# Layer norms transposed by VectorE, transfers and GpSimd in place of TensorE, in a two-layer cross-attention kernel

## The chip, the cores and the metric

One core of a Trainium2 chip runs the whole kernel. Its engines are named as in the profile: PE (TensorE, matrix products; PEld is its weight load), DVE (VectorE), ACT (ScalarE), POOL (GpSimd) and SP, whose queue issues nearly all transfers here. The metric is the device time of one execution in microseconds.

## The reference

Two transformer layers over x of 4 batches, 512 tokens and 320 features, with a context of 1601 tokens and 192 features per batch, all in 32-bit floats. Each layer does, for every batch:

```python
h1 = _ln(x, n1_g, n1_b)
x = _attn(h1, h1, q1, k1, v1, o1_w, o1_b, heads) + x
h2 = _ln(x, n2_g, n2_b)
x = _attn(h2, context, q2, k2, v2, o2_w, o2_b, heads) + x
h3 = _ln(x, n3_g, n3_b)
proj = h3 @ ff_w1 + ff_b1
a, g = jnp.split(proj, 2, axis=-1)
ff = a * jax.nn.gelu(g, approximate=False) @ ff_w2 + ff_b2
return ff + x
```

`_ln` subtracts the mean over the 320 features, divides by the standard deviation, and applies a gain and a bias per feature. `_attn` has 20 heads of 16 features: queries, keys and values are products, the scores are softmaxed over the keys, and the heads' outputs go through one more product. The feed-forward part has 2 x 1280 columns in its first product and 1280 rows in its second.

## The kernel before, in words

The work is cut into units in one fixed list: per layer, 20 self-attention units (4 batches by 5 groups of 4 heads), 20 cross-attention units, and 4 feed-forward units, one a batch. An attention unit goes through its keys in chunks of 128, 4 chunks in self and 13 in cross. For each chunk PE forms the scores of four heads (tile `st`, line 1185), ACT raises them to exponentials (`pr`, line 1195), and PE multiplies them with the values (`av`, line 1211); ACT copies the result out and POOL adds it up in `o` (line 1231). Each unit needs the largest score of every query beforehand: PE forms the scores a second time in another layout (`sps`, lines 959 and 986) and DVE takes their maxima (`pm` or `nmax`, lines 974 and 996). These products for the next units are woven into the score products of the present one, or are given out as extra rounds.

Everything else a unit needs (norms, projections of queries, keys and values, output products) stands in chains, queues of small steps with a cost and a due time counted in rounds. A round is half a chunk in attention. After each chunk `steps` takes the most urgent heads of the chains, as far as a credit allows. Steps marked `LIGHT` are limited to one or two at a time. The order of instructions on each engine is so written out when the program is built; on the chip every engine goes through its own list in order. Transfers of queries, keys and other things are queued and issued by `carry`, a few each round.

A layer norm is one run of the chain `norm`, 24 of them (2 layers, 3 places, 4 batches). DVE forms mean and variance of four tiles of 128 tokens (line 533), an inverse root is found by Newton steps on POOL (lines 503 to 513), DVE normalises each tile into `hn` (line 550), and then `turn` has PE transpose `hn` against an identity, three pieces of features by four tiles, 12 transposes a norm, into a PSUM bank `hps` (line 564). ACT reads each bank, applies gain and bias and writes `hT`, the normalised input with features on partitions (line 573). POOL adds the next product's bias to x (line 579). `hT` has two buffers; a buffer may be overwritten when the norm two before has been read by all its products (`may_overwrite`). For feed-forward norms the last 64 features are normalised twice, so that they lie on both halves of the partitions.

`hT` is the moving operand of the projections (lines 791, 832) and of the first feed-forward product (line 1314, and line 1328 for the last 64 features), and the stationary one for self-attention's values (line 920). The product that ends an attention (`ops`, line 1114) takes the heads' outputs `aT` by tiles of tokens.

The first cross unit of a layer is called early: its projections are put into the chains `AHEAD` = 8 units ahead, and its maxima are given out as extra rounds while self units still run (`giver`). In the last unit before the feed-forward part the next unit has no maxima, so ACT's exponentials set its pace.

Of the kernel before, what the change touches and what calls it, by code (L numbers as in the profile page):

```python
# [20 lines left out]
FF = 4 * D  # L21
# [13 lines left out]
DK = [(0, 0, 112), (1, 112, 112), (2, 224, 96)]  # L35
CK = [(0, 0, 96), (1, 96, 96)]
# [11 lines left out]
AHEAD = 8  # L48
# [5 lines left out]
REST = D - 2 * P  # L54
NAMES = (
# [18 lines left out]
def kernel(ctx: ExitStack, tc: tile.TileContext, x, context, ws, out):  # L74
# [83 lines left out]

    def take_weights():
        room["w1r"] = shared.tile([P, FF], F32, tag="rests", name="w1r")  # L160
        room["w2"] = shared.tile([P, NHC, D], F32, tag="second", name="w2")
# [19 lines left out]
    wqk = wpool.tile([P, 3, G, 2, GD], F32, name="wqk")  # L181
    wq1, wk1 = (wqk[:, :, :, i, :] for i in range(2))
# [22 lines left out]
    def load_rows(t, w, chunks):  # L205
        return [lambda k=k, at=at, n=n: dma(out=t[:n, k, :], in_=w[at : at + n, :]) for k, at, n in chunks]

    def load_columns(t, v, chunks):
        with nc.allow_non_contiguous_dma(reason="a vector's elements go to partitions"):
            for k, at, n in chunks:  # L210
                dma(out=t[:n, k : k + 1], in_=v[at : at + n].rearrange("(p o) -> p o", o=1))
# [10 lines left out]
    def load_norm(l, i):  # L222
        for t, v in ((lng[i], ws[l][f"n{i + 1}_g"]), (lnb[i], ws[l][f"n{i + 1}_b"])):
            load_columns(t, v, FK if i == 2 else DK)
# [4 lines left out]
    def load_self(l):  # L229
        return [lambda: load_norm(l, 0)] + [  # L230
            f for t, n in ((wq1, "q1"), (wk1, "k1"), (wv1, "v1")) for f in load_rows(t, ws[l][n], DK)
# [10 lines left out]
    def load_cross(l):  # L242
        def rows(t, w):
# [7 lines left out]
            + load_rows(wq2, ws[l]["q2"], DK)  # L251
# [4 lines left out]
    def load_ff(l):  # L256
# [5 lines left out]
        def last_rows(half):  # L262
            dma(
                out=room["w1r"][half * REST : (half + 1) * REST, :],
                in_=ws[l]["ff_w1"][2 * P :, half * FF : (half + 1) * FF],
# [4 lines left out]
            [small]  # L270
            + [lambda half=half: last_rows(half) for half in range(2)]
            + [lambda c=c: dma(out=room["w2"][:, c], in_=second[:, c]) for c in range(NHC)]
# [3 lines left out]
    def load_first(l):  # L276
# [3 lines left out]
            lambda k=k, at=at, c=c: dma(out=w1[:, k, c : c + n], in_=ws[l]["ff_w1"][at : at + P, c : c + n])  # L280
            for k, at, _ in FK
            for c in range(0, 2 * FF, n)
# [89 lines left out]
    chains = {n: deque() for n in ("divide", "project", "norm", "context", "early", "proj", "values")}  # L372
    clock = {"round": 0, "credit": 0.0, "lights": 0, "tiles": None}
# [141 lines left out]
    hn_used = []  # L515


    readers = []
# [5 lines left out]
    def add_norm(l, b, i, put, done, due):  # L524
# [20 lines left out]
        def normalise(t):  # L545
            if t == 0:
                s["hn"] = one.tile([P, NQ, D + REST], F32, tag="hn", name="hn")

            for to, at, n in ((0, 0, D), (D, D - REST, REST))[: 1 + i // 2]:
                nc.vector.tensor_scalar(  # L550
                    s["hn"][:, t, to : to + n], xb[:, t, at : at + n],
                    s["mv"][:, t, 0:1], s["rstd"][:, t : t + 1], ALU.subtract, ALU.mult,
                )
            busy("dve", 0.4 * (1 + i // 2))
            s["round"] = clock["round"]

        def turn(k, at, n):
            if k == 0:
                s["hT"] = two.tile([P, 3, N], F32, tag="hT", name="hT")
                readers.append(done)  # L560
            ps = bank("hps")
            n += REST if n == REST else 0
            for t in range(NQ):
                nc.tensor.transpose(ps[:n, t * P : (t + 1) * P], s["hn"][:, t, at : at + n], ident)  # L564
            written(0.5, ps)
            busy("act", 0.7, ps)
            if start["on"] and k == 1:
                nc.vector.tensor_scalar(
                    s["hT"][:n, k, :], ps[:n, :],
                    lng[i][:n, k : k + 1], lnb[i][:n, k : k + 1], ALU.mult, ALU.add,  # L570
                )
            else:
                nc.scalar.activation(
                    s["hT"][:n, k, :], ps[:n, :], AF.Identity,
                    bias=lnb[i][:n, k : k + 1], scale=lng[i][:n, k : k + 1],
                )
            for t in ((0,), (1,), (2, 3))[k]:

                nc.gpsimd.tensor_tensor(xb[:, t, :], xb[:, t, :], brow[(3 * l + i) % 2], ALU.add)
# [1016 lines left out]
```

## Time and profile before

| | us |
|---|---|
| runs, median of 3 | 3007.71 (3005.52 to 3010.42) |
| the profiled execution | 3006.85 |
| its span, first to last instruction | 3005.1 |
| PE busy | 2902.2 (97%) |
| DVE busy | 2115.8 (70%) |
| ACT busy | 1921.5 (64%) |
| POOL busy | 1158.6 (39%) |

The six stages, read from the times at which the groups of instructions change: self-attention of layer 0 up to 375 us, cross-attention up to 1236, feed-forward up to 1545; the same for layer 1 up to 1870, 2720 and 3005. In a row of a group of instructions, the line and engine come first, then what is written and read, the shapes and the count; after the bar the busy time and the mean duration of one, and after the next bar the idle time of the engine just before, with what ended it. In a row of the timeline the first number is the start and the second the time from the first start to the last end of a run of like instructions.

### The profile page before, as it was taken

The numbers are of one execution on the slowest core, as the hardware profiler recorded it, in microseconds if no ns is written. First come the engines' busy times: TensorE is split into PE (matmuls) and PEld (weight loads), VectorE is DVE, ScalarE is ACT, GpSimd is POOL, SyncE is SP. The second block draws the span as 40 slices with busy tenths as digits, with TensorE's granted clock in tenths as the row PEclk, the third lists the DMA queues.
The fourth block names the chain that finished last, engine by engine and source line by source line (L and its number), as shares of the span: only waits on it lengthen the run. The fifth ranks groups of instructions, "written<-read, shape, count | busy, mean of one in ns | idle before, by whom it ended". The sixth has DMA issues, their size and how long they took to land.

```text
span 3005.1 us, 84209 instructions
## 1 busy us (share of the span) xinstructions
PE 2902.2 (97%) x35210; PEld 1529.1 (51%) x35210; DVE 2115.8 (70%) x4061; ACT 1921.5 (64%) x3780; POOL 1158.6 (39%) x1257
## 2 busy tenths in 40 slices
PE   8999999999999999999999999999999999999999
PEld 4455554555554555455554555545545545544555
DVE  6877888888888888322257778888888888873221
ACT  3766677877877878511147666788778778784110
POOL 3444344454544444201124443444454444442000
PEclk9999999999999999999999999999999999999999
DMA  4454233132132121300123332221221121213000
GB/s 111 100 129 99 67 79 83 45 90 56 37 93 59 38 57 27 94 6 0 33 52 74 96 97 65 70 55 42 53 60 40 49 61 43 55 22 89 10 11 14
DMA packets 165548, 177.13 MB, mean 59 GB/s; under 512 B 72484, under 2 KB 116272, under 8 KB 165168
## 3 DMA queue, kind: packets, MB, share of 16 engines
q1 hardware_dynamic: 164376, 170.56, 22.5%
q8 instruction: 277, 4.54, 0.6%
q10 hardware_dynamic: 760, 1.18, 0.2%
q14 instruction: 103, 0.84, 0.1%
q0 software_dynamic: 32, 0.00, 0.0%
HBM read 55.76 MB, written 29.36 MB: 28 GB/s over the span
## 4 chain that ended last, share of the span: by engine, by line
PE 58%; DVE 8%; POOL 1%; issue 1%; ACT 0%; DMA 0%; SPq 0%; ACTq 0%; POOLq 0%; DVEq 0%
PE av L1211 14%; PE st L1185 10%; PE fps L1314 9%; PE yps L1371 6%; DVE pm L974 5%; PE sps L959 4%; PE vps L920 3%; PE fps L1328 2%; PE ops L1114 2%; PE kps L856 2%; PE qkps L791 2%; DVE nmax L974 2%; PE qps L832 1%; PE sps L986 1%; PE hps L564 1%
## 5 line engine op out<-in xcount | busy, mean ns | idle before, releaser
L1195 ACT ACTIVATE pr<-st 128x512 f32<-128x512 f32 (+1 forms) x2720 | 1404.8, 605 | 400.7 <-PE st L1185 359.4
L974 DVE TENSOR_REDUCE pm<-sps 128x1 f32<-128x512 f32 x1920 | 1186.9, 681 | 158.1 <-PE sps L959 150.1
L1231 POOL TENSOR_TENSOR o<-o,vo 128x512 f32<-128x512 f32 x576 | 740.3, 1285 | 1185.2 <-ACT vo L1230 1157.1
L959 PE MATMUL sps<-kT,q 32*128 32x512 f32 x4800 | 874.5, 429 | 15.2 <-DMA q<-low 5.6
L1211 PE MATMUL av<-pr,vals 128*32 128x512 f32 (+1 forms) x5440 | 738.2, 607 | 64.1 <-DVE pm L974 11.9
L1185 PE MATMUL st<-q,kT 32*128 32x512 f32 (+1 forms) x5120 | 783.7, 421 | 2.4 <-DVE pm L974 1.6
L1185 PEld LDWEIGHTS st<-q,kT 32*128 32x128 f32 (+1 forms) x5120 | 417.8, 180 | 273.1 <-issue 120.7
L1185 PE MATMUL st<-nrows,ones 32*128 32x512 f32 (+1 forms) x2720 | 539.3, 399 | 5.6 <-DMA nrows<-turned 5.6
L959 PEld LDWEIGHTS sps<-kT,q 32*128 32x128 f32 x4800 | 428.3, 184 | 95.0 <-DVE pm L974 19.2
L974 DVE TENSOR_REDUCE nmax<-sps 128x1 f32<-128x512 f32 x640 | 395.2, 681 | 84.7 <-PE sps L959 81.0
L1230 ACT COPY vo<-av 128x512 f32<-128x512 f32 x576 | 354.1, 615 | 33.8 <-PE av L1211 32.0
L1211 PEld LDWEIGHTS av<-pr,vals 128*32 128x32 f32 (+1 forms) x5440 | 111.7, 108 | 343.0 <-DVE pm L974 196.7
L1339 ACT ACTIVATE gl<-fps,b 128x512 f32<-128x512 f32 x80 | 54.7, 687 | 361.3 <-PE fps L1328 253.3
L1314 PE MATMUL fps<-hT,w 128*128 128x512 f32 x640 | 283.2, 596 | 0.0
L1185 PEld LDWEIGHTS st<-nrows,ones 32*128 32x128 f32 (+1 forms) x2720 | 246.3, 180 | 30.0 <-DMA nrows<-turned 3.9
L1340 DVE SCALAR_TENSOR_TENSOR hid<-fps,b,gl 128x512 f32<-128x512 f32 x80 | 59.7, 748 | 240.7 <-ACT gl L1339 238.5
L1314 PEld LDWEIGHTS fps<-hT,w 128*128 128x128 f32 x640 | 119.0, 190 | 150.4 <-issue 149.0
L1371 PE MATMUL yps<-w,hid 128*128 128x320 f32 x640 | 176.7, 435 | 0.0
L1371 PEld LDWEIGHTS yps<-w,hid 128*128 128x128 f32 x640 | 120.1, 190 | 55.5 <-ACT gl L1339 5.3
L1114 PEld LDWEIGHTS ops<-wo,aT 112*32 112x32 f32 (+1 forms) x3072 | 97.8, 110 | 62.1 <-issue 47.7
L1114 PE MATMUL ops<-wo,aT 112*32 112x160 f32 (+1 forms) x3072 | 124.7, 300 | 0.7 <-POOL aT L1096 0.7
L503 POOL TENSOR_SCALAR root<-root 128x4 f32<-128x4 f32 x22 | 5.0, 226 | 310.8 <-DVE root L497 310.1
(86 smaller groups left out, 2490.0 us busy)
## 6 DMA issues: line engine op xcount, KB each, us to landing
kT<-stages SPq DMA_DIRECT2D x160, 200.2 KB
oway<-o SPq DMA_DIRECT2D x80, 256.0 KB
q<-high SPq DMA_DIRECT2D x160, 64.0 KB
q<-low SPq DMA_DIRECT2D x160, 64.0 KB
kT<-high SPq DMA_DIRECT2D x60, 128.0 KB
q<-high SPq DMA_DIRECT2D x60, 128.0 KB
kT<-low SPq DMA_DIRECT2D x57, 128.0 KB
aT<-oway SPq DMA_DIRECT2D x32, 224.0 KB
```

The lines of the kernel that those rows point to most:

```text
L791: nc.tensor.matmul(ps[f : f + m, :w], lhsT=columns[:, f : f + m], rhs=first.hT[:n, k, at : at + w], start=(k == 0), stop=(k == 2),)
L920: nc.tensor.matmul(ps[f : f + m, :w], lhsT=u.kvT[:n, k, at + f : at + f + m], rhs=wv[:n, k, h0 * DH : h1 * DH], start=(k == 0), stop=(k == ...
L959: nc.tensor.matmul(ps, lhsT=u.q[j * SLOT : (j + 1) * SLOT, e, t * P : (t + 1) * P], rhs=u.kT[j * SLOT : (j + 1) * SLOT, u.k0 + s * 512 : u ...
L974: nc.vector.tensor_reduce(to[:, j : j + 1], ps, AX.X, ALU.max, negate=(ns == 1))
L1114: nc.tensor.matmul(ps[f : f + m, : D // 2], lhsT=aT[:n, k, t * P + f : t * P + f + m], rhs=wo[:n, k, cols], start=(k == 0), stop=(k == 2),)
L1185: nc.tensor.matmul(own[0][:r, :], lhsT=ones[rows, :r] if e == 2 else u.keys(rows, c), rhs=u.rows[rows, :] if e == 2 else u.q[rows, e, :], ...
L1195: nc.scalar.activation(p[:r], own[0][:r], AF.Exp)
L1211: nc.tensor.matmul(ps[j * SLOT : (j + 1) * SLOT, :], lhsT=columns_of[:r, head : head + SLOT], rhs=pr.pop((c, j))[:r, :], start=True, stop= ...
L1230: nc.scalar.copy(vo, ps)
L1231: nc.gpsimd.tensor_tensor(u.o, u.o, vo, ALU.add)
L1314: nc.tensor.matmul(ps, lhsT=w1[:, k, i * FF + c * P : i * FF + (c + 1) * P], rhs=u.hT[:, k, :], start=ahead and k == 0, stop=not ahead and ...
L1371: nc.tensor.matmul(ps[:, :D], lhsT=hid[c][:, t * P : (t + 1) * P], rhs=w2[:, c, :], start=(c == 0), stop=(c == NHC - 1),)
```

## The change: what it does

20 of the 24 norms no longer use PE. DVE normalises a tile of 128 tokens into `hn` and transposes it there and then in blocks of 32 by 32 into `turned`. A block transpose leaves each block of features on the 32 partitions of its tokens' band, so transfers move the bands to their places in `hT`: 4 bands by 3 pieces, 12 transfers a norm (16 for a feed-forward norm, whose last 64 features go to both halves). They are queued in `bands` and `carry` issues at most three a round, six during the feed-forward part. In `hT` the features of a piece are then in another order, and so are the tokens; weights, gains and biases are loaded with their rows in the same order, and the feed-forward and output products read the tokens through a view that puts them right. After a piece has had time to land, POOL applies gain and bias in place (`affine`), a new chain `scale`. These norms start 14 rounds sooner in attention. Four norms keep the transposes on PE, those of self-attention of batches 0 and 1 in layer 0 and of cross-attention of batch 0 in both layers; `plain` writes their features in the new order.

The early cross unit is put into the chains 10 units ahead, its context one unit sooner. In self units the first extra round stands behind the values of the chunk before. Four products of the first feed-forward unit are issued in the last chunk of the last cross unit (`begin`), and this unit starts with the last pair of its ten column blocks. Weights of the feed-forward part are loaded in another order, some of them one or two units sooner.

```diff
+HK = [(0, 0, P), (1, P, 96), (2, P + 96, 96)]
...
-AHEAD = 8
+AHEAD = 10
...
     def load_rows(t, w, chunks):
-        return [lambda k=k, at=at, n=n: dma(out=t[:n, k, :], in_=w[at : at + n, :]) for k, at, n in chunks]
+        return [
+            lambda k=k, at=at, n=n: dma(out=t[:n, k], in_=w[at : at + n, :].rearrange("(k d) c -> d k c", d=SLOT))
+            for k, at, n in chunks
+        ]
...
+    EARLIER = 14
+    LANDS = (4, 2)
+    bands = deque()
...
         def normalise(t):
             if t == 0:
-                s["hn"] = one.tile([P, NQ, D + REST], F32, tag="hn", name="hn")
...
+                s["turned"] = one.tile([P, DB, NQ, SLOT], F32, tag="hturned", name="hturned")
+            s["hn"] = one.tile([P, D], F32, tag="hn", name="hn")
+            nc.vector.tensor_scalar(
+                s["hn"], xb[:, t, :], s["mv"][:, t, 0:1], s["rstd"][:, t : t + 1], ALU.subtract, ALU.mult,
+            )
+            busy("dve", 0.4)
+
+        def blocks(t):
+            nc.vector.transpose(s["turned"][:, :, t, :], s["hn"])
+            busy("dve", 0.45)
+            s["round"] = clock["round"]
...
+        def move(part, band):
+            k, k0, n, to = part
+            dma(
+                out=s["hT"][to : to + n, k, band * P : (band + 1) * P],
+                in_=s["turned"][band * SLOT : (band + 1) * SLOT, k0 : k0 + n // SLOT].rearrange("p k t w -> p k (t w)"),
+            )
...
+        def affine(k, n):
+            nc.gpsimd.tensor_scalar(
+                s["hT"][:n, k], s["hT"][:n, k], lng[i][:n, k : k + 1], lnb[i][:n, k : k + 1], ALU.mult, ALU.add,
+            )
+            s["scaled"] = clock["round"]
...
+        def plain(t):
+            if t == 0:
+                s["hn"] = one.tile([P, DB, NQ, SLOT], F32, tag="hturned", name="hturned").rearrange("p k t w -> p (k t w)")
+            for k, at, n in HK:
+                w = n // SLOT
                 nc.vector.tensor_scalar(
-                    s["hn"][:, t, to : to + n], xb[:, t, at : at + n],
+                    s["hn"][:, t * D + at : t * D + at + n].rearrange("p (d k) -> p k d", k=w),
+                    xb[:, t, at : at + n].rearrange("p (k d) -> p k d", k=w),
                     s["mv"][:, t, 0:1], s["rstd"][:, t : t + 1], ALU.subtract, ALU.mult,
                 )
...
+        first = i == 0 and b < 2 and l == 0 or i == 1 and b == 0
+        ahead = 0 if first or i == 2 else EARLIER
+        parts = [(0, 0, P, 0), (1, 4, 96, 0), (2, 7, 96, 0)]
...
+        for t, f in enumerate(together(lambda t: (normalise(t), blocks(t)))):
+            add("norm", LIGHT, f, due - ahead - 13 + t, yes, yes if t else later(1))
+        add("norm", 0.0, spread, due - ahead - 6, may_overwrite, later(1))
...
+        def landed(k):
+            return lambda: clock["round"] >= moved[k] + LANDS[i == 2] and clock["round"] > s.get("scaled", 0)
+
+        for k, n in enumerate((P, P, P) if i == 2 else (P, 96, 96)):
+            add("scale", 0.0, lambda k=k, n=n: affine(k, n), due - 6 + k, there(k), landed(k))
+        add("scale", 0.0, lambda: put(s["hT"]), due - 2, yes, later(1, "scaled"))
...
+        few = 6 if clock["ff"] else min(room + 1, 3)
+        while bands and few > 0 and clock["round"] >= bands[0][0]:
+            bands.popleft()[1]()
+            few -= 1
...
-            if extra:
+            if extra and u.cross:
                 round_of(extra[0])
             flush()
             late.append(lambda c=c: values(c))
+            if extra and not u.cross:
+                round_of(extra[0])
+            if last and c == u.nch - 1:
+                for _ in range(4):
+                    begin(units[u.i + 1])
...
+    def natural(tokens):
+
+        return tokens.rearrange("p (i t w) -> p t i w", t=NQ, w=SLOT)
...
+    ORDER = (NHC - 2,) + tuple(range(0, NHC - 2, 2))
+    begun = []
+
+    def begin(u):
+
+        if len(begun) == 2 * len(FK):
+            return
+        i, k = divmod(len(begun), len(FK))
+        if k == 0:
+            until_normed(lambda: u.hT is not None)
+            begun.append(bank("fps"))
+        else:
+            begun.append(begun[-1])
+        first_layer(u, ORDER[0], i, k, begun[-1], k == 0, False)
+        written(0.86, begun[-1])
...
-    EARLY = 7
+    EARLY = 6
```

More of the change, by code (lines that the diff above doesn't have):

```diff
@@ L364 @@
         ]
-    chains = {n: deque() for n in ("divide", "project", "norm", "context", "early", "proj", "values")}
-    clock = {"round": 0, "credit": 0.0, "lights": 0, "tiles": None}
+    chains = {n: deque() for n in ("divide", "project", "norm", "scale", "context", "early", "proj", "values")}
+    clock = {"round": 0, "credit": 0.0, "lights": 0, "tiles": None, "ff": False}
     ALIKE = ("project", "early", "proj", "values")
@@ L607, with until_normed @@
+    def until_normed(test):
+        while not test():
+            if chains["scale"] and chains["scale"][0][2]():
+                run("scale")
+            elif bands:
+                bands.popleft()[1]()
+            else:
+                run("norm")
     CGRP = [(c0, min(2, NC2 - c0)) for c0 in range(0, NC2, 2)]
@@ L1357, in ff_main @@
                     beside(ahead and not e, 2)
-                full(c + e, pss[e], not ahead)
+                if e or not some:
+                    full(c + e, pss[e], not ahead)
             these, pss = pss, None
@@ L1559 @@
             loads.clear()
[L1560 removed]
+            until_normed(lambda: u.hT is not None)
+        clock["ff"] = u.kind == "ff"
         add_norms(i)
```

167 lines of the change are left out of this document (102 added, 65 removed).

## The prediction

> **What bounds the kernel now.** I read the page's totals and its chain of work, then the busy time by stage, then the groups of instructions that the change touches.
>
> ```profile
> span 3005.1 us, 84209 instructions
> ## 1 busy us (share of the span) xinstructions
> PE 2902.2 (97%) x35210; PEld 1529.1 (51%) x35210; DVE 2115.8 (70%) x4061; ACT 1921.5 (64%) x3780; POOL 1158.6 (39%) x1257
> ...
> PE 58%; DVE 8%; POOL 1%; issue 1%; ACT 0%; DMA 0%; SPq 0%; ACTq 0%; POOLq 0%; DVEq 0%
> ```
>
> PE is busy nearly all the time, and the chain runs mostly through it; DVE is the only other engine on it. By stage (self, cross and feed-forward of layer 0, then of layer 1):
>
> ```profile
> 0.00:375.00 375.00, 351.76 (x4978) 190.47 (x4982) 290.84 (x601) 240.14 (x478) 157.68 (x184) 0.98 0.41 101
> 375.00:1236.00 861.00, 828.17 (x11608) 432.41 (x11608) 716.03 (x1347) 685.50 (x1365) 398.47 (x383) 1.00 0.25 64
> 1236.00:1545.00 309.00, 308.12 (x1543) 162.19 (x1540) 88.82 (x190) 51.44 (x80) 44.60 (x98) 1.00 0.07 19
> 1545.00:1870.00 325.00, 311.26 (x4512) 169.71 (x4504) 253.79 (x495) 226.97 (x451) 138.07 (x156) 0.99 0.35 85
> 1870.00:2720.00 850.00, 821.17 (x11508) 428.24 (x11512) 704.32 (x1303) 676.59 (x1347) 396.96 (x382) 1.00 0.21 54
> 2720.00:3006.00 286.00, 281.70 (x1084) 146.12 (x1078) 62.04 (x126) 40.88 (x62) 22.83 (x54) 1.00 0.06 18
> ```
>
> The columns are length, PE, PEld, DVE, ACT and POOL busy, PE clock, DMA share, GB/s. In the two feed-forward stages PE leaves no gap (308.1 of 309) and DVE works under a third of the time: PE work taken away there is time taken away. In the four attention stages (2411 us) PE is 92 to 97% busy and DVE 78 to 83%: PE first, DVE close behind.
>
> **The change part by part.** *Transposes leave TensorE.* There are 24 norms of 12 transposes each. Four keep them (layer 0 self with batches 0 and 1, and batch 0 of cross in each layer); 20 lose them.
>
> ```profile
> L564 PE MATMUL hps<-ident,hn 128*112 128x128 f32 (+2 forms) x288 | 41.8, 279 | 1.9 <-DVE hn L550 1.8
> ...
> L573 ACT ACTIVATE hT<-hps,lnb,lng 112x512 f32<-112x512 f32 (+2 forms) x71 | 53.3, 788 | 62.9 <-PE hps L564 62.7
> ```
>
> Neighbours overlap, so I take busy over count, 41.8 / 288 = 0.145 us, not the 279 ns of one. 240 x 0.145 = **34.9 us off PE**: 12 norms (20.9) inside attention, 8 (13.9) while the feed-forward runs (its own batches 1 to 3 in both layers, and layer 1's self norms of batches 0 and 1). ACT loses 60 x 0.788 = 47 us; it is not on the chain, so 0.
>
> *What DVE gets.* Each of the 20 norms adds four block transposes of 128x320.
>
> ```profile
> L550 DVE TENSOR_SCALAR hn<-x,mv,root 128x320 f32<-128x320 f32 x96 | 57.6, 622 | 22.5 <-POOL root L513 22.4
> ...
> L550 DVE TENSOR_SCALAR hn<-x,mv,root 128x64 f32<-128x64 f32 x32 | 18.6, 580 | 0.0
> ...
> L1028 DVE STREAM_TRANSPOSE turned<-parts 128x32 f32<-128x32 f32 x80 | 16.9, 212 | 3.1 <-DMA rT<-rway 0.4
> ...
> L642 DVE STREAM_TRANSPOSE stages<-stages 128x192 f32<-128x192 f32 x52 | 16.5, 353 | 0.0
> ```
>
> From 212 ns at 32 columns to 353 at 192 is 0.88 ns a column, so 466 ns at 320: 80 x 0.466 = 37.3 us. 14.9 of it runs beside the feed-forward, where DVE has room (and 32 copies of the 64 last columns, 18.6 us, go). 48 x 0.466 = 22.4 us fall in attention. The ends: nothing, or all 22.4 if DVE binds. The chain is 8% DVE, 240 of the 2411 us of attention, which would make 2.2; cross is fuller than the mean, so I take **+5**. The four norms that stay on PE are normalised in three pieces a tile, 48 instructions for 16; only the very first norm stands bare, about 8 more pieces of 0.2 us, **+1.5** (ends 0 and 8: 16 tiles by 0.5).
>
> *What GpSimd and the transfers get.* Three scale-and-shift instructions a norm on POOL, 60 in all, and 12 transfers (16 for a feed-forward norm), 12 x 12 + 8 x 16 = 272 more or less, on SP's queue, at most three a round in attention and six in feed-forward. No such POOL operation is in the trace of before; it lies between these two:
>
> ```profile
> L709 POOL TENSOR_TENSOR low<-low,high 128x512 f32<-128x512 f32 x39 | 49.9, 1279 | 3.1
> ...
> L708 POOL CAST high<-low 128x512 fp32r<-128x512 f32 x39 | 24.0, 617 | 113.3 <-ACT low L807 106.6 <-DMA q<-high 5.9 <-DMA q<-low 0.8
> ```
>
> Between 37 and 77 us (one input, so nearer the cast: 37) on an engine that is 39% busy: 0 on the path. For transfers:
>
> ```profile
> 264.13 2.90 SPq L757 DMA_DIRECT2D kT<-stages  x4
> ```
>
> ```profile
> q1 hardware_dynamic: 164376, 170.56, 22.5%
> ...
> nrows<-turned POOLq DMA_DIRECT2D x1, 4.0 KB, 1.9
> ```
>
> An issue takes 0.7 us of SP (2.90 / 4), so a norm fills SP for 8 to 12 us, spread over four or more rounds; the head and query moves behind it are late by at most three issues, 2 us, and have rounds to spare. The bytes are 20 x 640 KB and more, 8% on top of queue 1's 171 MB, whose packets took 22.5% of the engines. A scaling that stands on POOL before its transfer has landed would hold up the sums of o and the splits of queries and keys behind it, and through the splits the moves; the rounds it is kept back are there for that. I put all this at 0. What hides it is that a norm now begins 14 rounds sooner. A cross round is 861 / 520 = 1.66 us (20 units of 13 chunks, two rounds each), so that is 23 us. The new steps after the last block transpose are 1 + 4 + 4 + 3 + 1 = 13 rounds: one to start, four of three transfers, four to land, three scalings, one to hand over. It fits by one round; without that cover every waiting product pays (the second rival).
>
> *First cross unit's maxima sooner.* Its projections are enqueued ten units ahead in place of eight, its context one unit sooner. Its maxima now begin at 306 us:
>
> ```profile
> L974 DVE TENSOR_REDUCE pm<-sps x51: 649/680/693, 305.9 to 379.4; 128x1 f32<-128x512 f32 x51
> L996 DVE TENSOR_REDUCE pm<-sps x4: 418/426/430, 366.5 to 372.0; 128x4 f32<-128x260 f32 x4
> ```
>
> ```profile
> 250.00:300.00 50.00, 48.79 (x771) 28.14 (x762) 33.50 (x66) 33.62 (x68) 27.41 (x26) 1.00 0.46 115
> 300.00:350.00 50.00, 49.27 (x564) 24.53 (x560) 46.97 (x88) 34.93 (x69) 14.34 (x12) 1.00 0.24 62
> ```
>
> From 300 to 350 DVE is full (47.0 of 50) and PE, busy by its row, gets 564 products in where it got 771: it is held back. In the 50 us before, DVE has 16.5 us free. If the maxima begin 20 us sooner, at that free share (33%) 6.6 us of DVE work leave the full stretch: 0 to 7 us a layer. What makes it less than 7 is that batch 0's norm still has to wait for its x and for one of two hT buffers. I take 2.5 a layer, **-5** (ends 0 and -14).
>
> *Four products sooner.* They go between the last unit's last scores and its last values, where PE waits for the exponentials:
>
> ```profile
> 1231.32 1.13 PE L1211 MATMUL av<-pr,vals 128*32 128x512 f32 x8
> ...
> 1233.22 3.32 PE L1211 MATMUL av<-pr,vals 128*32 128x512 f32 x16
> ```
>
> Sixteen should take 2.26 and took 3.32: a gap of 1.06 us a layer is filled, **-2.1** (ends 0 and the eight instructions whole, 2 x 8 x 0.44 = -7, from the first row below).
>
> *Order in self units.* The extra maxima go behind the values, not ahead of them.
>
> ```profile
> PE av L1211 <- DVE nmax L974: 9.0, 5, 3.3
> ```
>
> Values waited 9.0 us for these maxima in all; most is one stall that has another cause (below): **-1**, ends 0 and -9.
>
> *Views.* Feed-forward products read hT in runs of 32 tokens, since transfers leave the tokens in bands; the loads of weights permute rows but keep them whole.
>
> ```profile
> L1314 PE MATMUL fps<-hT,w 128*128 128x512 f32 x640 | 283.2, 596 | 0.0
> ...
> L1328 PE MATMUL fps<-hT,w1r 64*128 64x512 f32 x320 | 75.2, 605 | 0.0
> ```
>
> No row reads such a view, so nothing bounds it from above; each 1% is 3.6 us of these 358. I take 0: the number of columns streamed is the same. A penalty of 10% would undo the whole forecast. Weights w1 ordered sooner, the den tile in another pool: 0, PE never waited for them.
>
> **The sum.** -34.9 + 5 + 1.5 - 5 - 2.1 - 1 = -36.5. The profiled execution took 3006.85 us (span 3005.1), 0.9 under the median shown: 3006.85 - 36.5 = **2970.3 us**.
>
> **A rule against it.** GpSimd is given work while DVE is. This is what one does to the other now, in the self stage of layer 1:
>
> ```profile
> 1660.56 1.29 POOL L709 TENSOR_TENSOR low<-low,high 128x512 f32<-128x512 f32 x1
> ...
> 1660.74 1.13 DVE L501 TENSOR_SCALAR root<-root 128x4 int32<-128x4 int32 x1
> ```
>
> A four-column DVE operation took 1.13 us and ended with the POOL one. The Trainium skill, "SBUF — State Buffer", section "SBUF: two separate sides", says that DVE and GpSimd share a port pair as an exclusive lock, so that the loser blocks for the whole instruction; the trace agrees (1.13 us). By it alone the 60 new POOL instructions could hold DVE for up to their whole length. That is the first rival's second half; the block transposes themselves keep to 353 ns in the mean.
>
> **The rivals.** *DVE takes PE's place in attention (0.18).* For it: 47.0 of 50 us at 300 to 350, and 83% in cross. Against: the chain is PE 58% to DVE 8%. Then only the feed-forward share counts, 13.9 + 2.1: 2990.8 us; with POOL's 37 us of locks falling on DVE a third of the time, up to 3003.
>
> *The turned norm comes late (0.16; slower).* A norm's readers stand in PE's queue in program order, so a late hT stops everything behind it. The place is the hold ahead of a batch's first projection, the price this:
>
> ```profile
> 1671.38 1.94 PE L1211 MATMUL av<-pr,vals 128*32 128x512 f32 x8 [3.32 <-DVE nmax L974]
> ```
>
> ```profile
> 1660.00:1670.00 10.00, 7.01 (x88) 3.37 (x80) 7.53 (x13) 7.52 (x15) 9.10 (x19) 1.00 0.65 174
> 1670.00:1680.00 10.00, 8.54 (x100) 4.07 (x104) 6.96 (x16) 4.08 (x8) 1.29 (x2) 0.83 0.33 84
> ```
>
> There POOL's root steps were late, DVE's normalising behind them, and PE idled 3.32 us, after which its clock was 0.83 for 10 us: some 5 us (3.0 + 1.5 of idle in the rows, and the slower clock). The Trainium skill, "TensorE: Matmul & The Clock Gate", section "Why this matters for your kernels", warns of gaps above about 3 us for this reason; the trace agrees. It decides from 36.5 / 20 = 1.8 us a norm; if each of the 12 attention norms lost 5 us, 60 in all, the time is 3030.
>
> *The early maxima do not begin sooner (0.25 within the forecast's case).* Then 2975.
>
> **How the numbers follow.** The forecast, 2955 to 2985 on its own, has 0.60, DVE's rival 0.18, a wash between them 0.06, the late norm 0.16. About 0.2% (6 us) is what a measurement of this kernel tells from no change. Faster: 0.60 + 0.18 = 0.78; same 0.06; slower 0.16. All gains at their far ends make -34.9 - 14 - 7 - 9 = -65, 2942; DVE's rival ends at 3003. Range 2945 to 3006.
>
> **What would show it.** Right: 48 transposes left on PE; 240 fewer PE instructions; feed-forward stages about 7 us shorter each; cross stages 5 to 7 each; 80 DVE transposes near 0.47 us; 60 POOL scalings near 0.6; maxima of the first cross unit beginning before 306. Wrong: PE waiting for GpSimd's scaling of hT, the clock below 1.00 in more stretches than before, or DVE's busy share above 90% in cross with a longer stage.

## The result, and the profile after

The changed kernel takes 3010.7 us (median) against 3007.1 of the kernel before, a ratio of 1.0011 with a 95% interval of 1.0004 to 1.0017. The forecast was 2970.3. The profiled execution took 3011.88 us, its span 3010.1. The page's totals and its chain:

```profile
span 3010.1 us, 84343 instructions
PE 2898.5 (96%) x34970; PEld 1511.8 (50%) x34970; DVE 2151.0 (71%) x4138; ACT 1880.0 (62%) x3723; POOL 1201.2 (40%) x1317
...
PE 77%; DVE 17%; POOL 2%; issue 1%; DMA 1%; ACT 1%; SPq 1%; POOLq 0%; ACTq 0%; DVEq 0%
```

PE has its 240 instructions fewer, yet its busy time fell by 3.7 us only (2902.2 before). DVE has 17% of this chain and had 8% of the one before, but the two shares cannot be set side by side: the chain of before adds up to 68%, because it was followed back no further than this piece:

```profile
951.16 1.11 PE av L1211 x8
```

From 951 us on, the pieces that DVE has on the chain add up to 249 us before (12% of that stretch) and 283 us after (14%). Stage by stage, cut so that each stage ends at the same event as before (columns as in the prediction):

```profile
0.00:391.00 391.00, 361.41 (x4906) 190.85 (x4908) 302.90 (x631) 235.37 (x471) 162.15 (x190) 0.95 0.40 100
391.00:1258.00 867.00, 835.34 (x11621) 432.87 (x11617) 721.08 (x1360) 678.64 (x1355) 407.31 (x395) 0.99 0.26 67
1258.00:1558.00 300.00, 299.75 (x1526) 156.61 (x1523) 94.69 (x198) 41.15 (x67) 50.43 (x108) 1.00 0.13 31
1558.00:1883.00 325.00, 306.98 (x4386) 163.20 (x4385) 262.64 (x512) 220.97 (x441) 147.85 (x168) 0.98 0.37 90
1883.00:2733.00 850.00, 821.34 (x11528) 427.33 (x11532) 707.59 (x1315) 672.47 (x1344) 404.90 (x394) 1.00 0.23 58
2733.00:3010.00 277.00, 273.71 (x1020) 140.98 (x1013) 62.08 (x125) 31.45 (x47) 28.55 (x63) 1.00 0.09 25
```

Against 375, 861, 309, 325, 850 and 285 us before (2720 to the end of the span): the first self stage lost 16, the first cross stage 6; the feed-forward stages gained 9 and 8; the second layer's attention is where it was. The groups that the change touched:

```profile
L621 PE MATMUL hps<-ident,hturned 128*96 128x128 f32 (+1 forms) x48 | 7.0, 282 | 4.2 <-DVE hturned L608 2.7 <-DVE nmax L1069 1.5
```

```profile
L562 DVE TENSOR_SCALAR hn<-x,mv,root 128x320 f32<-128x320 f32 x80 | 52.6, 657 | 19.3 <-POOL root L523 17.9
L568 DVE STREAM_TRANSPOSE hturned<-hn 128x320 f32<-128x320 f32 x80 | 40.9, 512 | 2.8
L595 POOL TENSOR_SCALAR hT<-hT,lng,lnb 128x512 f32<-128x512 f32 x36 | 27.7, 770 | 125.8 <-DMA hT<-hturned 114.2 <-PE ops L1209 11.6
L595 POOL TENSOR_SCALAR hT<-hT,lng,lnb 96x512 f32<-96x512 f32 x24 | 18.4, 768 | 23.6 <-DMA hT<-hturned 23.6
```

The operations are there in the numbers and near the prices forecast (512 ns a block transpose for 466; 769 ns a scaling, 46 us for 60, inside 37 to 77). What was lost is not their sum but where they stand, as the runs below show. To place it, I followed when each attention unit issues its output transfer (`oway<-o`), unit by unit, counted from 0 within a stage. A jump is by how much more a unit is behind the kernel before than the unit ahead of it was. Three jumps stand out in the changed kernel.

**Unit 3, first self stage: 5.3 us.** DVE and PE (start, duration, line, in brackets the idle time ahead):

```profile
103.55 1.38 DVE L562 TENSOR_SCALAR hn<-x,mv,root 128x320 f32<-128x320 f32 x1 [1.63 <-POOL root L523]
104.96 0.51 DVE L568 STREAM_TRANSPOSE hturned<-hn 128x320 f32<-128x320 f32 x1
105.51 0.45 DVE L562 TENSOR_SCALAR hn<-x,mv,root 128x320 f32<-128x320 f32 x1
105.99 0.51 DVE L568 STREAM_TRANSPOSE hturned<-hn 128x320 f32<-128x320 f32 x1
106.43 2.45 DVE L1069 TENSOR_REDUCE nmax<-sps 128x1 f32<-128x512 f32 x4
```

```profile
107.14 0.50 PE L1280 MATMUL st<-kT 32*128 32x512 f32 x2 [1.26 <-DVE nmax L1069]
```

Two tiles of batch 2's norm stand in one go on DVE, 2.9 us, ahead of the maxima whose banks PE is waiting for. Of the 5.3 us, 1.26 show as this wait; the clock was 0.88 and 0.78 in the two stretches of 5 us from 105 us on, about 1.7 us by estimate (5 x 0.12 + 5 x 0.22). The rest is not placed.

**Unit 8, first self stage: 9.3 us.** The output transfers of units 7 and 8, before and after:

```profile
183.61 0.56 SPq L1055 DMA_DIRECT2D oway<-o  x1
192.86 0.58 SPq L1055 DMA_DIRECT2D oway<-o  x1
```

```profile
197.14 0.56 SPq L1150 DMA_DIRECT2D oway<-o  x1
215.70 0.61 SPq L1150 DMA_DIRECT2D oway<-o  x1
```

SP's queue after, and what waited:

```profile
197.81 0.58 SPq L741 DMA_DIRECT2D ctxT<-stages  x1
203.68 2.89 SPq L755 DMA_DIRECT2D w<-ctxT  x4
...
208.54 0.59 SPq L852 DMA_DIRECT2D q<-low  x1
209.18 0.62 SPq L578 DMA_DIRECT2D hT<-hturned  x1
209.84 2.52 SPq L755 DMA_DIRECT2D w<-ctxT  x4
212.41 0.60 SPq L852 DMA_DIRECT2D q<-high  x1
213.05 0.60 SPq L852 DMA_DIRECT2D q<-low  x1
```

```profile
215.56 0.84 ACT L902 ACTIVATE low<-qkps,scales 128x256 f32<-128x256 f32 x2 [7.85 <-DMA hT<-hturned]
```

```profile
PE sps L1054 <- ACT low L902: 5.6, 1, 5.6
```

```profile
205.00:210.00 5.00, 4.88 (x80) 2.49 (x74) 2.92 (x7) 2.54 (x5) 0.00 (x0) 1.00 0.80 210
210.00:215.00 5.00, 0.50 (x10) 0.07 (x2) 1.29 (x2) 0.00 (x0) 0.00 (x0) 0.96 0.76 206
215.00:220.00 5.00, 3.92 (x26) 1.74 (x30) 1.29 (x2) 3.22 (x7) 1.88 (x2) 0.50 0.40 76
```

The queue waits 5.2 us for a write of the context to land, and the last moves of queries leave at 213 us. ACT waits 7.85 us before it fills `low`, the buffer from which those moves read, and PE waits 5.6 us for ACT. The profile names a band transfer of the same queue as what ended ACT's wait; that it was the moves is read from the program (ACT's instruction does not touch `hT`) and not shown by the trace. The next 5 us run at a clock of 0.50, which by estimate costs 2.5 us more, about half the stall again.

**Unit 18 of both cross stages: 5.7 and 5.8 us.**

```profile
1185.46 4.26 DVE L1069 TENSOR_REDUCE pm<-sps 128x1 f32<-128x512 f32 x7
1190.14 1.39 DVE L562 TENSOR_SCALAR hn<-x,mv,root 128x320 f32<-128x320 f32 x1 [0.42 <-POOL root L523]
...
1194.65 0.51 DVE L568 STREAM_TRANSPOSE hturned<-hn 128x320 f32<-128x320 f32 x1
1195.09 4.84 DVE L1069 TENSOR_REDUCE pm<-sps 128x1 f32<-128x512 f32 x8
```

```profile
1195.80 1.32 PE L1280 MATMUL st<-q,kT 32*128 32x512 f32 x4 [2.42 <-DVE pm L1069]
```

The feed-forward norm of batch 0, which the change starts two units sooner, does its four scalings and four block transposes back to back, 4.95 us (1190.14 to 1195.09), between maxima. The rows are those of layer 0.

### The profile page after: what moved, and what is told of

The parts are those of the page before. It is cut to its first block, busy times and chain, and to the rows that moved or that the text cites. A ratio compares the mean times of both kernels' runs of the same rounds, so it can differ in the third digit from the quotient of the medians.

```text
span 3010.1 us, 84343 instructions
## 1 busy us (share of the span) xinstructions
PE 2898.5 (96%) x34970; PEld 1511.8 (50%) x34970; DVE 2151.0 (71%) x4138; ACT 1880.0 (62%) x3723; POOL 1201.2 (40%) x1317
## 4 chain that ended last, share of the span: by engine, by line
PE 77%; DVE 17%; POOL 2%; issue 1%; DMA 1%; ACT 1%; SPq 1%; POOLq 0%; ACTq 0%; DVEq 0%
PE av L1306 21%; PE st L1280 15%; PE fps L1391 9%; DVE pm L1069 8%; PE sps L1054 6%; PE yps L1498 6%; PE vps L1015 5%; PE ops L1209 3%; PE kps L951 3%; DVE nmax L1069 3%; PE qkps L886 2%; PE fps L1451 2%; PE qps L927 2%; PE sps L1081 1%; DVE hn L562 1%
## 5 line engine op out<-in xcount | busy, mean ns | idle before, releaser
L1280 PE MATMUL st<-q,kT 32*128 32x512 f32 (+1 forms) x5120 | 799.3, 422 | 14.9 <-DVE pm L1069 10.7
L1280 PEld LDWEIGHTS st<-nrows,ones 32*128 32x128 f32 (+1 forms) x2720 | 247.3, 180 | 31.1 <-DMA nrows<-turned 7.5
L1505 DVE TENSOR_TENSOR x<-yps,x 128x320 f32<-128x320 f32 x32 | 15.7, 491 | 146.3 <-PE yps L1498 146.3
```

The lines of the kernel that those rows point to most:

```text
L1280: nc.tensor.matmul(own[0][:r, :], lhsT=ones[rows, :r] if e == 2 else u.keys(rows, c), rhs=u.rows[rows, :] if e == 2 else u.q[rows, e, :], ...
```

## The experiments

Each is timed against the kernel before, on the same chip; ratios have their 95% interval. "The changed kernel" is at 3010.7 us. The runs lie on more than one chip, on which the kernel before read 3006.6 to 3007.6 us, so a difference between two runs of about 1 us says nothing.

**The early maxima by themselves.** In the kernel before:

```diff
-AHEAD = 8
+AHEAD = 10
-    EARLY = 7
+    EARLY = 6
```

> The kernel before with only the lead of the first cross unit changed (AHEAD 10 for 8, EARLY 6 for 7). Theory, that the early maxima are worth what the stretch from unit 11 to unit 14 of the self stages showed in the changed kernel (6 to 7 us a layer): about 2995 us, 12 less than before, all of it between those two units. Rival, that this stretch only caught up what the stalls ahead of it had put off: between 3002 and 3007 us. A third, that bringing the context a unit sooner is what stops unit 8 in the changed kernel: the first layer's unit 8 is late by 8 us here too, and the total is 3003 to 3010.

3000.3 us, 0.9978 (0.9969 to 0.9987): 6.5 us, half of the theory's 12. From unit 11 to 14 of the first self stage it gained 5.8, but by unit 10 it had lost 6.8; that this is because the context comes a unit sooner was not tested apart. Unit 8 was 5.7 late, so both the first and the third expectation hold in part. The second self stage did the same (5.7 lost, 6.3 gained), and the net gain came in the cross stages, 3.3 and 3.7 us. It is near the prediction's -5.

**All attention norms on PE.** In the changed kernel:

```diff
-        first = i == 0 and b < 2 and l == 0 or i == 1 and b == 0
+        first = i < 2
```

> The changed kernel with all 16 norms of the attention stages turned by TensorE in the new plain form; the feed-forward norms and all else stay. Theory, that the turned norms cost the self stages more than they give: the delays of unit 3 (5.3 us) and unit 8 (9.3 us) of the first layer and 4 us of the second layer's self stage go, the 240 - 96 transposes that come back cost up to 20.9 us and the cross stages lose 5 us each: 3000 to 3012 us. Rival, that the turned norms give their 20.9 us and the delays have other causes: about 3030 us.

3024.0 us, 1.0054 (1.0040 to 1.0067): between the two. The first self stage ended 10.8 us sooner than in the changed kernel (unit 8 stood at +5.3 against before, for +22.8), and all later attention stages were slower. So the turned norms pay as a whole, and the delays of the first self stage come with them.

**The feed-forward norm, spread.** Its batch 0 one tile in a round:

```diff
+        slow = i == 2 and b == 0
...
-        for t, f in enumerate(together(lambda t: (normalise(t), blocks(t)))):
-            add("norm", LIGHT, f, due - ahead - 13 + t, yes, yes if t else later(1))
+        for t, f in enumerate([lambda t=t: tiles(t) for t in range(NQ)] if slow else together(tiles)):
+            add("norm", LIGHT, f, due - ahead - 13 + t, yes, yes if t and not slow else later(1))
```

> The changed kernel with the first feed-forward norm of each layer (batch 0) done one tile in a round, and not two tiles at a time with two turns in one round. Theory, that its four scalings and four block transposes in one go (4.95 us of VectorE ahead of the maxima) are the 5.7 us that each layer loses at its last cross units: 2999 to 3001 us, and unit 18 of both cross stages is early by 5 us against the changed kernel. Rival, that the delay comes with the transfers or the loads of weights at that place: 3009 to 3012 us.

3006.4 us, 0.9996 (0.9987 to 1.0005): 4 us, not 10. Unit 18 still lost 4.0 and 4.2 us. That the work stands in one go is the smaller part there.

**The start.** The first two norms by column groups:

```diff
-            for t in range(NQ):
-                add("norm", LIGHT, lambda t=t: plain(t), ...)
...
+            for k, at, n in HK:
+                add("norm", LIGHT, lambda k=k, at=at, n=n: columns(k, at, n), ...)
```

> The changed kernel with the first two norms of the program made column group by column group (four pieces of one group for all tiles, then the next), so that the first transposes of TensorE wait for 4 pieces and not for 12. Theory, that the 3.39 us of pieces, for 1.51 before, and the slower clock that follows are the 4.9 us of the start: about 3006 us, with the first unit's end 4 to 5 us sooner. Rival, that the clock of the start is set by the later wait for the second norm's pieces (also 3.39 us, which stay): not more than 1.5 us, 3009 us.

3012.0 us, 1.0014 (1.0006 to 1.0023): no gain. The first unit's end came 3.2 us sooner in the profiled execution, but in kernels whose start was not touched it lay anywhere from 0.5 to 4.9 us behind the kernel before. The start's loss is not settled, and it is small.

**The feed-forward norm back in the last unit**, without the four products ahead:

```diff
-        ... norms[0].i <= i + ((1 if norms[0].b else 3) if norms[0].kind == "ff" ...
+        ... norms[0].i <= i + (1 if norms[0].kind == "ff" ...
...
-                for _ in range(4):
+                for _ in range(0):
                     begin(units[u.i + 1])
```

> The changed kernel with the first feed-forward norm of each layer put back into the last cross unit, and so without the four products that begin ahead of the feed-forward stage. Theory, that VectorE is full while it takes the maxima of the last units (4.7 to 4.9 us busy of each 5), so that the 7 us of this norm cost what they last there, however they are spread (spreading them gave back 1.5 us a layer), and are free in the last unit, which has no maxima to take: the 5.7 us of each layer's unit 18 go, 2.1 come back with the four products: 3003 us against 3010.7. Rival, that the norm then ends too late and the feed-forward stage waits for it: the 5.7 us go and 6 or more come back at the start of the stage, 3010 us or more.

2999.2 us, 0.9974 (0.9964 to 0.9985): 11.5 us less than the changed kernel. Unit 18's loss is gone in both layers. The feed-forward stages gave back 3.6 and 1.9 us. Both parts of the change were undone together, so this is what the four products and the earlier norm were worth there: more than the 2.1 forecast, and less than the earlier place cost.

**Bands behind moves.**

```diff
-        few = 6 if clock["ff"] else min(room + 1, 3)
+        few = 6 if clock["ff"] else 3 if room == 4 else 0
```

> The changed kernel with band transfers issued in the attention stages only in those rounds in which no move of heads was issued. Theory, that the bands stand ahead of the moves on SP's queue and that this is the 9 us that unit 8 of the first layer loses: about 3003 us. Rival, that the queue stands there for the context's round trip (5.2 us of waiting in one place, against 0.65 us for the one band issued between the moves): 3010 to 3012 us, with unit 8 as late as before.

3007.4 us, 1.0000 (0.9992 to 1.0009): 3 us, between the two. In the profiled execution unit 8 was 11 us sooner, but that execution was the quickest of its kernel; the median does not bear it out.

**The context, turned a unit sooner.**

```diff
-        ... u.kind == "self" and u.m == EARLY - 2:
+        ... u.kind == "self" and u.m == EARLY - 3:
...
+        if u.kind == "self" and u.m == EARLY - 1 and u.l == 0:
+            add_turned(0, u.start + 22, 2)
...
-            if u.l == 0:
-                add_turned(0, u.start + 22, 2)
```

> The changed kernel with the first context of the first layer loaded and turned one unit sooner, and its loads from memory left where they are, so that they need not wait for the last write. Theory, that SP's wait of 5.2 us for that write, with eight loads of 0.63 us and the moves behind it, is what stops unit 8: its 5.6 us of waiting go, unit 8 is 5 to 9 us sooner and the total 3002 to 3006 us. Rival, that the bands and moves are what hold the queue: 3010 to 3012 us. Against both: the turning then meets units 4 to 6, and could cost there what it cost at 7 and 8.

3015.8 us, 1.0028 (1.0018 to 1.0039). Unit 8 itself lost 0.4 us in place of 9.3, but units 5 to 7 lost 17.6, with one wait of PE of 7.0 us for ACT's `low`. The stall moved with the context's work.

**One tile in a round.** For the attention stages' turned norms:

```diff
+        slow = i < 2
...
-            add("norm", LIGHT, f, due - ahead - 13 + t, yes, yes if t else later(1))
+            add("norm", LIGHT, f, due - ahead - 13 + t, yes, yes if t and not slow else later(1))
```

> The changed kernel with the turned norms of the attention stages done one tile (scaling and block transpose, about 1.2 us) in a round, where two may fall into one round. Theory, that the pairs of tiles ahead of the maxima are the 5.3 us of the first layer's unit 3: unit 3 is 3 to 5 us sooner, and a few us come in the second layer's self stage: 3003 to 3007 us. Rival, that VectorE has no room in these units however the work is spread: 3009 to 3012 us.

2991.0 us, 0.9945 (0.9933 to 0.9958): 19.6 us, far more than the theory had. Unit 8's jump went too (it stands 7.8 behind the kernel before, for 22.8), so it is fed by the pairs as well as by the context. By the units' ends, 12 of the profiled execution's 19 us came in the first self stage and 7 in the first cross stage; the second layer gained under 1.

**Pairs, over the same four rounds.**

```diff
-            add("norm", LIGHT, f, due - ahead - 13 + t, yes, yes if t else later(1))
+            add("norm", LIGHT, f, due - ahead - 13 + t, yes, (yes if i == 2 else later(3)) if t else later(1))
```

Here `f` holds two tiles, by an edit of the loop around this line.

> The changed kernel with the tiles of the attention stages' turned norms done two at a time (scaling, block transpose, scaling, block transpose, about 2.4 us of VectorE in one go), the second pair three rounds behind the first, so that the four tiles take the same four rounds, and the bands leave in the same round, as with one tile in a round, which took 2991.0 us. Theory, that the pair ahead of the maxima is what costs: as slow as the changed kernel, 3005 to 3011 us. Rival, that the gain came from the bands, moves and scalings that follow being a few rounds later: 2990 to 2995 us.

3002.3 us, 0.9984 (0.9975 to 0.9992). Of the 19.6 us, pairs in one go cost 11.2 (3002.3 - 2991.0), and the four rounds, whatever is in them, give 8.4. Both are at work, and neither expectation holds. The split is rough: this kernel forces pairs in rounds where the changed kernel may allow one tile only.

**Both mends together**: one tile in a round, and the feed-forward norm in the last unit.

> The changed kernel with one tile in a round for the attention stages' turned norms, and the first feed-forward norm back in the last cross unit without the four products ahead. Alone the first gave 19.6 us and the second 11.5 against the changed kernel. Theory, that the two losses lie at different places (norms of the attention stages; last two cross units): they add to 2979 to 2982 us. Rival, that they overlap or that the planner's order shifts: 2985 to 2991 us.

2980.2 us, 0.9909 (0.9895 to 0.9923). They add (19.6 + 11.5 = 31.1; 30.4 measured).

**And bands behind moves**, as above:

> As the kernel with one tile in a round and the norm in the last unit, with band transfers only in rounds that issued no move of heads. Theory, that the bands still stand ahead of moves now and then, as the 3 us say that this edit gave alone: 2 to 4 us less than that kernel. Rival, that those 3 us were part of the same delays of the first layer's self stage, which are gone: within 2 us of it.

2998.1 us, 0.9966 (0.9953 to 0.9979): 18 us worse. PE's wait for the self stages' maxima, without the edit and with it:

```profile
PE av L1308 <- DVE nmax L1071: 14.9, 9, 4.5
```

```profile
PE av L1308 <- DVE nmax L1071: 19.2, 13, 4.6
```

Four microseconds of 18 show there. By the units' ends, the two profiled executions, 12.9 us apart, differ in the cross stages (10.5 and 5.6 us lost). The bands need their places in the rounds; how most of it is lost stays open.

**One light piece in a round**, on top of both mends:

```diff
-            steps(None, 1 if extra or c == u.nch - 1 else 2)
+            steps(None, 1)
```

> As the kernel with one tile in a round and the norm in the last unit, with one light piece of work in every round of the attention stages where two were allowed, so that statistics, roots, reciprocals and context turns are spread too. Theory, that any burst of VectorE ahead of the maxima costs: 2 to 8 us less than that kernel. Rival, that these pieces (0.3 to 0.7 us each) fit into the slack, or come too late when spread: the same or slower by up to 10 us.

2974.2 us, 0.9892 (0.9876 to 0.9908), the best kernel of the study, 33 us faster than the kernel before. Its profile has the same 34970 PE instructions as the changed kernel:

```profile
PE 2877.0 (97%) x34970; PEld 1509.5 (51%) x34970; DVE 2131.3 (72%) x4117; ACT 1882.4 (63%) x3744; POOL 1200.6 (40%) x1317
```

PE is busy 21.5 us less for the same products, and its idle time is 95.3 us for 111.6. Busy PE on the page is time and not work: it holds the products that ran at a lower clock, of which this kernel has fewer (below). The place that corresponds to unit 3 above:

```profile
105.37 0.44 DVE L562 TENSOR_SCALAR hn<-x,mv,root 128x320 f32<-128x320 f32 x1
105.84 0.51 DVE L568 STREAM_TRANSPOSE hturned<-hn 128x320 f32<-128x320 f32 x1
107.27 2.48 DVE L1071 TENSOR_REDUCE nmax<-sps 128x1 f32<-128x512 f32 x4 [0.92 <-PE sps L1056]
109.67 0.44 DVE L562 TENSOR_SCALAR hn<-x,mv,root 128x320 f32<-128x320 f32 x1
110.15 0.51 DVE L568 STREAM_TRANSPOSE hturned<-hn 128x320 f32<-128x320 f32 x1
```

One tile, then maxima; DVE now waits for PE (0.92), not PE for DVE.

**Is pacing a gain of its own?** The same two limits in the kernel before, and the second with the early maxima; and the second alone in the changed kernel:

> The kernel before with its normalise steps (one tile, 0.38 us) one in a round, as in the run of the changed kernel that gave 19.6 us. Theory, that this spacing gave back a cost which only the changed kernel has (1.2 us a tile with the block transpose): within 3 us of the kernel before. Rival, that spacing the norm is a gain of its own, and the changed kernel lost less by its pairs than 19.6 us: 8 to 20 us less than before.

> The kernel before with one light piece of work in every round of the attention stages. Theory, that spreading gains only where pieces are long: within 4 us of the kernel before. Rival, that the 6 us which it gave on top of the mended kernel were never the change's: 5 to 10 us less than before.

> The changed kernel with one light piece of work in every round and nothing else. It keeps two tiles in one piece for the first feed-forward norm, and tiles of one norm fall into successive rounds. Theory, that bursts of VectorE are the loss of the self and cross units: 2984 to 2992 us, the 5 us at each layer's unit 18 remaining. Rival, that the gap between a norm's steps matters and not the burst: 3000 us or more.

> The kernel before with the first cross unit's lead as changed (3000.3 us alone) and one light piece of work in a round: all that the best kernel so far (2974.2 us) has, without the turned norms and with the old layouts. Theory, that turning the norms is worth what is left: 2994 to 3002 us, so 20 to 28 us for the norms in both stages. Rival, that the turned norms of the attention stages give little and pacing gives most: 2980 to 2988 us.

The kernel before with one tile in a round: 3006.6 us, 0.9998 (0.9989 to 1.0007), nothing. With one light piece: 3003.2, 0.9988 (0.9979 to 0.9997), 3.4 us. The changed kernel with one light piece and nothing else: 2985.6, 0.9929 (0.9916 to 0.9941), 25 us less than the changed kernel. The kernel before with early maxima and one light piece: 3007.8, 1.0000 (0.9991 to 1.0009), above both expectations and 7.5 more than with early maxima alone, so there the two do not add. The pacing mends what the change brought; the kernel before has little to mend. From 3007.8 to 2974.2 lie 33.6 us, and from the fastest kernel with all norms on PE (3000.3, early maxima alone) 26.1. The difference is the turned norms and new layouts, but also the change's order in self units and its order of weights and column blocks, which no run takes apart.

## Why the prediction was wrong, step by step

- *Transposes leave TensorE, -34.9*: the instructions went (48 left, 7.0 us). The gain was real: 26.1 to 33.6 us from the kernels with all norms on PE to the best one with turned norms, by which of the two above one starts; this includes what DVE gets (the prediction's three terms make -34.9 + 5 + 1.5 = -28.4). From the paced one, stage ends put 34.7 of it into cross (20.4 and 14.3) and 13.4 into feed-forward; the self stages lost 14 (3.3 and 11.1).
- *What DVE gets, +5, ends 0 to 22.4*: **the step that failed.** I priced 48 block transposes by DVE's share of the chain, as if they were spread evenly. The share was misread too: the 8% of the span, 249 us, come from a chain that starts at 951 us, and 239 us of them lie in the 1460 us of attention behind that, 16%, which would have made 3.7 us and not 2.2. But no share could have given the cost. A tile became 0.96 us (0.45 + 0.51, undisturbed) in place of 0.44 for a scaling alone, two tiles could share a round, and the kernel takes maxima on DVE round after round. One tile in a round, which moves nothing but these norms, gave back 19.6 us, so the cost was near the upper end of 22.4 or past it, and it was a cost of order, not of work. One light piece in a round, which also spreads statistics, roots and turns of the context, gave 25.1 (the kernel before gets 3.4 us from the same limit). And the prediction missed that batch 0's feed-forward norm was moved two units ahead, out of the one unit in which DVE takes no maxima: another 11.5 us (11.4 from 2985.6 to 2974.2). 25.1 + 11.5 = 36.6 of the 40.4 us between forecast and measurement.
- *Plain norms, +1.5*: not resolved; the first unit's end varies by 4 us between profiled executions of kernels with the same start.
- *GpSimd and transfers, 0*: no wait of PE for a scaling is among PE's largest in the changed kernel. Nor did POOL's scalings hold DVE up, as the first rival had it: all 80 block transposes took 511 to 514 ns, and a maximum 680 ns in the mean as before (681). "Late by at most 2 us, with rounds to spare" was too kind at unit 8, where the queue was already waiting for the context.
- *First cross unit's maxima sooner, -5*: near, -6.5 alone, but partly by luck: in both self stages a loss that the sum did not have ate the gain, and the net came in the cross stages. The fall from 771 to 564 products, read there as PE held back, is largely another mix: 192 products of 160 columns stand in the first of the two stretches and none in the second. The mark I named (beginning before 306 us) fell, at 306.7, since the whole stage was 20 us late.
- *Four products sooner, -2.1*: 3.6 and 1.9 us in the feed-forward stages together with the earlier norm, at the price above.
- *Order in self units, -1*, and *Views, 0*: not tested apart. The first feed-forward product took 597 ns for 596, so its view of 32-token runs cost nothing here.
- *DVE takes PE's place*, the rival at 0.18, had the mechanism but the wrong size: the feed-forward stages gave 16.4 us (8.8 and 7.6) for the 16.0 that it counted on, but the attention stages gave all that back and more. *The turned norm comes late* did not happen.
- The marks for "wrong" included a clock below 1.00 in more stretches. That is what the traces show: 28 stretches of 5 us within the span below 1.00 in the changed kernel, 12 before, 15 in the best one. The Trainium skill, "TensorE: Matmul & The Clock Gate", section "Why this matters for your kernels", says that PE-idle gaps of more than about 3 us bring the slow clock; the trace agrees at unit 8 (0.50 after a 5.6 us wait), and shorter waits were followed by a lower clock too: 0.76 after 2.4 us at unit 18, 0.88 and 0.78 around the 1.26 us at unit 3.

The best kernel stands at 2974.2 us, 3.9 from the number forecast, without the four products and with a limit that the prediction did not have, so that the nearness of the two numbers confirms no single term. Its stages:

```profile
0.00:384.00 384.00, 354.29 (x4942) 188.07 (x4946) 299.43 (x630) 237.65 (x482) 162.92 (x191) 0.98 0.40 102
384.00:1226.00 842.00, 817.79 (x11579) 429.24 (x11572) 709.52 (x1347) 678.11 (x1362) 402.15 (x390) 1.00 0.27 68
1226.00:1528.00 302.00, 301.74 (x1528) 157.35 (x1526) 94.85 (x197) 41.15 (x67) 54.35 (x113) 1.00 0.13 33
1528.00:1855.00 327.00, 313.15 (x4416) 166.80 (x4414) 264.56 (x517) 221.70 (x443) 148.17 (x168) 0.98 0.36 89
1855.00:2694.00 839.00, 815.11 (x11496) 426.30 (x11496) 699.33 (x1305) 672.00 (x1345) 400.45 (x389) 0.99 0.22 57
2694.00:2972.00 278.00, 274.95 (x1024) 141.71 (x1020) 63.63 (x125) 31.84 (x48) 32.51 (x68) 1.00 0.10 29
```

Cross 842 and 839 us (861 and 850 before), feed-forward 302 and 278 (309 and 285), self 384 and 327 (375 and 325). The feed-forward stages gave the 7 us each that were forecast. The cross stages gave 19 and 11 where 5 to 7 were forecast, and the self stages lost. Self and cross of a layer taken together are 10 and 9 us shorter; how much of this is work that moved from one stage to the other is not shown.

## What to carry to other kernels

When work moves to an engine that hands out a result in every round, price the longest uninterrupted stretch that it can form ahead of that result, not its share of the engine's time; then look in the code for what allows two such pieces into one round. When a step is moved earlier to make room for its successor, read the busy rows of the place that it lands in. And test a loss by pacing the same work before taking it out: here a one-line limit gave 25 us, and turned a loss of 3.5 us against the kernel before into a gain of 21.

## What the hardware showed that I had not expected

A DVE scaling that started beside a POOL sum did not end before the sum: 1.38 and 1.39 us in the rows above, 0.44 to 0.45 in the others there. The Trainium skill, "SBUF — State Buffer", section "SBUF: two separate sides", describes a port pair shared by DVE and GpSimd as an exclusive lock, held for the whole instruction by whichever starts first; the trace agrees that the scaling is held until the sum ends. Both scalings end 0.18 us after the sum, less than the 0.44 us of one alone; what they did before that is not shown. The POOL rows beside those two:

```profile
103.31 0.20 POOL L523 TENSOR_TENSOR root<-root,root 128x4 f32<-128x4 f32 x1
103.47 1.28 POOL L1326 TENSOR_TENSOR o<-o,vo 128x512 f32<-128x512 f32 x1
...
1190.06 1.29 POOL L1326 TENSOR_TENSOR o<-o,vo 128x512 f32<-128x512 f32 x1
```

New to me is how it depends on order: the same 80 scalings took 657 ns in the mean in the changed kernel and 494 in the best one, which spreads them:

```profile
L562 DVE TENSOR_SCALAR hn<-x,mv,root 128x320 f32<-128x320 f32 x80 | 39.5, 494 | 9.2 <-POOL root L523 8.1
```

In the two rows above, the norm's first scaling waits for POOL's last root step, and POOL's next instruction is such a sum, so the two meet.
